# A two-layer graph network on one core: the first layer's own half kept in DRAM and normalised a stage later

## The chip, the cores and the metric

The kernel runs on one core of a Trainium2 chip. The metric is device time in microseconds (us), lower is better. Engines are named as in the profile: PE (matmul) and PEld (its weight loads), DVE (vector), ACT (scalar), POOL (GpSimd) and SP (which only issues DMAs here).

## What is computed

The inputs are x of 12,500 rows by 256, a list of 200,000 edges (src, dst, sorted by dst) with a weight each, and the weights of two layers. Each layer adds its output to x and applies a layer norm. The first layer, cut to what matters here:

```
feat = relu(einsum('nd,ohdk->ohnk', x, W) + b)      # o=0: own half, o=1: neighbour half
att_s = leaky(sum_k feat[0] * a_self)               # 4 heads of 32
att_n = leaky(sum_k feat[1] * a_neigh)
edge_w = (att_s[:, src] + att_n[:, dst]) * weight
agg    = segment_sum(edge_w * feat[1][:, dst], src)
per half and head: (f - mean) * scale * rsqrt(var + 1e-9) + offset
x = layernorm(x + concat(own, agg))
```

The second layer gathers a projected row for each edge, adds the projection of the edge's dst row, applies ReLU, sums by dst, and ends in a matmul, two norms and a residual.

## The kernel before

The edges are cut into tiles of 128, the tiles into 112 groups of 14 (NG = 112, GT = 14). As the edges are sorted by dst, all dst rows of a group lie in one window of 128 rows of x. The nodes are also cut into 98 fixed blocks of 128 rows (NB = 98). Three stages follow each other.

**First stage** (lines 218 to 840). For each group, `sort_tasks` sorts its edges by the block of their src: one-hots of the block of each of the 14 tiles (`widen`, `hot`, `hot_b`, a tile A of 128 x 14 x 99 in bf16), counts per block (`ranks`, 14 matmuls with a column of ones, L600), first rows and places (`begins`, 14 matmuls more, L615; `place_mm`, `place_pick`, L667), and one-hots that permute the edges (`hot_q`, `hot_r`, `goods`, `permute`). The order goes out to DRAM and comes back to all partitions (`rel_out`, `rel_in`, `hot_n`, L725). `message` and `evict` (L734, L741) build a row for each edge from F3, the neighbour half in three bf16 parts, and `scatter` (L747) writes the rows to a log in DRAM, four indirect DMAs a group. The rows lie in a tile m, of which there are three.

For each group, `feat_tasks` makes the features. The neighbour half is needed for the group's window (`xw`), the own half for the block g (`xb`), while there are blocks. So 98 of the 112 steps transpose four squares (L446, L449), copy 512 columns (L455), project both halves from different rows (L467), and then, for the own half, also compute its norm: `offsets` (L460), `square` (L522), `var` (L526), `root` (L529), `rstd` (L532), `norm` (L536), `scale` (L540), `put` (L543). `out_y` stores x + offset + own half in `yd`. The own attention stays in the SBUF tile `atts`.

**The order of the stage is written out by hand.** The table AT gives every task a position; a task of group g stands at 256 g + AT[name]; all tasks are sorted by position and issued in that order. Each engine works through its own instructions in this order, and waits only where data or a buffer is not ready. The `m_` tasks prepare eight groups at a time (their edges' indices and weights).

**Middle stage** (912 to 1116). For each block, its log rows are read in five tiles (`log_load`, `log_hot`, `log_sum`); tile t is summed two steps after its one-hots are made (L958 on DVE, from four `o2` buffers; the multiply L953 on POOL, each fifth tile on DVE; matmuls L966). Log loads are issued nine steps ahead. Blocks are finished in batches of four (the first ones of 1 and 3, the last ones smaller): `load_y` reads the batch's `yd`, `heads_a` to `heads_d` norm the aggregated half (L980 to L1016), then come the layer norm's statistics (L1022), the projection (L1045 to L1059) and the stores. A step is a tile; a batch's tasks stand at steps counted from its first block (b NK, NK = 5) or its end.

**Third stage** (1130 to the end): the second layer, with gathers by POOL (L1286).

Of the kernel before, what the change touches and what calls it, by code (L numbers as in the profile page):

```python
# [11 lines left out]
def _warn_once_fixed(msg, *args, **kwargs):  # L12
# [28 lines left out]
    "widen": -140, "hot": -47, "hot_b": 3, "ranks": 44, "quarter": 71, "rows": 78, "begins": 155,  # L41
    "keep_begins": 189, "keep_v": 180, "shift": 218, "reach": 377, "steps": 314, "steps_keep": 337,
    "steps_low": 358, "target": 474, "index": 554, "place_mm0": 207, "place_mm1": 281, "place_mm2": 370,
    "pick0": 224, "pick1": 255, "pick2": 256, "pick3": 299, "pick4": 305, "pick5": 305, "pick6": 312,
    "pick7": 368, "pick8": 401, "pick9": 408, "pick10": 435, "pick11": 456, "pick12": 457, "pick13": 481,
    "split": 523, "hot_r": 547, "goods": 577, "hot_q": 563, "permute": 636, "rel_keep": 663, "extras": 717,
    "rel_turn": 685, "rel_row": 708, "rel_out": 738, "rel_in": 884, "hot_n": 885, "message0": 965,
    "evict0": 985, "message1": 1004, "evict1": 1046, "message2": 1006, "evict2": 1074, "message3": 1051,
    "evict3": 1132, "message4": 1092, "evict4": 1150, "message5": 1140, "evict5": 1200, "scatter0": 1078,
    "scatter1": 1124, "scatter2": 1163, "scatter3": 1210, "load": -363, "transposes": 234, "keep": 250,  # L50
    "project": 290, "relu": 308, "offsets": 441, "att_mult": 334, "mean_sum": 371, "att_sum": 404,
    "centre": 388, "leaky_n": 494, "part0": 507, "part1": 678, "part2": 741, "part3": 780, "leaky_s": 899,
    "square": 476, "var": 595, "root": 656, "rstd": 792, "norm": 814, "scale": 916, "put": 941, "out_y": 1139,
    "m_load": -1372, "m_cast0": -982, "m_cast1": -1209, "m_col0": -970, "m_keep0": -940, "m_col1": -414,
    "m_keep1": -359, "m_col2": -655, "m_keep2": -607, "m_block": -852, "m_place": -776, "m_high": -348,
    "m_rest": -26, "m_mid": 2, "m_low": 358, "m_win": -179, "m_turn": -654, "m_pairs": -648, "m_mask": -313,
    "m_count": 101,
# [45 lines left out]
def kernel(  # L103
# [45 lines left out]
    yd = dram.tile([ROWS, D], FT, name="yd")  # L149
# [12 lines left out]
    atts = consts.tile([P, NB, H], FT, name="atts")  # L162
# [55 lines left out]
    with ExitStack() as l0:  # L218
# [195 lines left out]
        xb = {}  # L414
        F3 = {}

        def load_group(g):
            if g < NG:
                b = base_reg(g) if g else 0
                xw[g] = xin.tile([P, D], FT, name="xw")  # L420
                nc.sync.dma_start(xw[g], x[bass.ds(b, P), :])
            if g < NB:
                xb[g] = xin.tile([P, D], FT, name="xb")
                n = min(P, N - g * P)
                if n < P:
                    nc.vector.memset(xb[g], 0.0)
                nc.sync.dma_start(xb[g][:n], x[g * P:g * P + n, :])

        def feat_tasks(g):

            ww, bb = g < NG, g < NB
            o0, o1 = (0 if bb else 1), (2 if ww else 1)
            lo, hi = o0 * HD, o1 * HD
            st = {}

            def flat(t):
                return t[:, lo:hi]

            def heads(t):
                return t[:, lo:hi].rearrange("p (a k) -> p a k", k=32)  # L440

            def transposes():
                tp = ps.tile([P, 512], FT, name="tp", bufs=1)
                if ww:
                    for c in range(2):
                        nc.tensor.transpose(tp[:, c * P:(c + 1) * P], xw[g][:, c * P:(c + 1) * P], ident)  # L446
                if bb:
                    for c in range(2):
                        nc.tensor.transpose(tp[:, (2 + c) * P:(3 + c) * P], xb[g][:, c * P:(c + 1) * P], ident)  # L449
                st["tp"] = tp  # L450

            def keep():
                xT = feat.tile([P, 4, P], FT, name="xT")
                a, z = (0 if ww else 2), (4 if bb else 2)
                nc.scalar.copy(xT[:, a:z].rearrange("p c q -> p (c q)"), st["tp"][:, a * P:z * P])  # L455
                st["xT"] = xT

            def offsets():
                st["y"] = feat.tile([P, D], FT, name="y", bufs=3)
                nc.vector.tensor_tensor(st["y"], xb[g], ofb, op=OP.add)  # L460

            def project():
                fp = bank[g][:, 0:D] if ww else ps.tile([P, 512], FT, name="fs")[:, 0:D]
                nc.tensor.matmul(fp[:, lo:hi], ones3, bias3[:, lo:hi], start=True, stop=False)
                for o in range(o0, o1):
                    for c in range(2):
                        nc.tensor.matmul(  # L467
                            fp[:, o * HD:(o + 1) * HD], st["xT"][:, (2 + c) if o == 0 else c, :],
                            w0s[:, c, o * 4:(o + 1) * 4, :].rearrange("p a k -> p (a k)"),
                            start=False, stop=(o == o1 - 1 and c == 1))  # L470
                st["fp"] = fp

            def relu():
                st["R"] = feat.tile([P, D], FT, name="R")
                nc.scalar.activation(flat(st["R"]), st["fp"][:, lo:hi], AF.Relu)

            def att_mult():
                st["tm"] = feat.tile([P, D], FT, name="tm")
                nc.vector.tensor_tensor(flat(st["tm"]), flat(st["R"]),
                                        atb.rearrange("p o h k -> p (o h k)")[:, lo:hi], op=OP.mult)  # L480

            def mean_sum():
                st["m"] = feat.tile([P, 2 * H], FT, name="m")
                nc.vector.tensor_reduce(st["m"][:, o0 * H:o1 * H], heads(st["R"]), AX.X, OP.add)

            def att_sum():
                st["a"] = feat.tile([P, 2 * H], FT, name="a")
                nc.vector.tensor_reduce(st["a"][:, o0 * H:o1 * H], heads(st["tm"]), AX.X, OP.add)

            def centre():  # L490
                st["F"] = feat.tile([P, D + H], FT, name="F", bufs=4)
                m = st["m"][:, o0 * H:o1 * H]
                nc.vector.scalar_tensor_tensor(
                    heads(st["F"]), m[:, :, None].to_broadcast([P, (o1 - o0) * H, 32]), -1.0 / 32, heads(st["R"]),
                    op0=OP.mult, op1=OP.add)

            def leaky_n():
                a = st["a"][:, H:2 * H]
                nc.vector.scalar_tensor_tensor(st["F"][:, D:D + H], a, 0.2, a, op0=OP.mult, op1=OP.max)


            def part(k):
                def f():
                    n = st["F"][:, HD:]
# [11 lines left out]
            def leaky_s():  # L516
                a = st["a"][:, 0:H]
                nc.vector.scalar_tensor_tensor(atts[:, g, :], a, 0.2, a, op0=OP.mult, op1=OP.max)

            def square():  # L520
                st["q"] = feat.tile([P, HD], FT, name="q")
                nc.scalar.activation(st["q"], st["F"][:, 0:HD], AF.Square)  # L522

            def var():
                st["v"] = feat.tile([P, H], FT, name="v")
                nc.vector.tensor_reduce(st["v"], st["q"].rearrange("p (h k) -> p h k", h=H), AX.X, OP.add)  # L526

            def root():
                nc.scalar.activation(st["v"], st["v"], AF.Sqrt, bias=epsh, scale=1.0 / 32)  # L529

            def rstd():
                nc.vector.reciprocal(st["v"], st["v"])  # L532

            def norm():
                c = st["F"][:, 0:HD].rearrange("p (h k) -> p h k", h=H)
                nc.vector.tensor_tensor(c, c, st["v"][:, :, None].to_broadcast([P, H, 32]), op=OP.mult)  # L536

            def scale():
                c = st["F"][:, 0:HD]
                nc.vector.tensor_tensor(c, c, scb[:, 0:HD], op=OP.mult)  # L540

            def put():
                nc.vector.tensor_tensor(st["y"][:, 0:HD], st["y"][:, 0:HD], st["F"][:, 0:HD], op=OP.add)  # L543

            def out_y():
                nc.sync.dma_start(yd[g * P:(g + 1) * P, :], st["y"])

            w = lambda f: f if ww else None
            k = lambda f: f if bb else None
            return dict(transposes=transposes, keep=keep, project=project, relu=relu, offsets=k(offsets),  # L550
# [253 lines left out]
        for g in range(max(NG, NB)):  # L804
            t0 = TG * g
            if g < NG:
                for name, f in sort_tasks(g).items():
                    put_in(t0, name, f)
# [808 lines left out]
```

## Time and profile before

| | |
|---|---|
| Median of 3 runs | 4087.51 us (4082.6 to 4089.36) |
| Profiled execution, its own time | 4089.95 us |
| Its span, first to last instruction | 4088.2 us |
| Mean granted PE clock | 0.989 |
| Busy, share of the span | PE 88%, PEld 74%, DVE 78%, ACT 60%, POOL 62% |
| DMA | 763.85 MB, mean 187 GB/s |

The profile tells for each engine when it was busy, for each group of instructions (line, operation, tile out<-in) the count, the busy time, the mean duration and the idle time just before with what ended it. "L522" is line 522 of the kernel before. A line such as "x98 | 29.9, 306 | 0.0" reads: 98 instructions, 29.9 us busy in all, 306 ns each, no idle time before them.

### The profile page before, as it was taken

The page shows a single profiled execution, that of the slowest core. Times are in us where ns is not written, and L with a number is a line of the kernel's source. Part 1 is how long each engine was busy: PE and PEld are TensorE (multiplying, and loading weights), DVE is VectorE, ACT ScalarE, POOL GpSimd, SP SyncE. Part 2 cuts the span into 40 slices and gives each one's busy share as a digit, 9 for nine tenths or more (in the row PEclk, how much of TensorE's full clock was granted, in tenths as well). Part 3 has the DMA queues.
Part 4 walks back from the last instruction along what each step waited for, and adds up shares of the span by engine and source line. Part 5 has one row for each costly group of instructions (what it writes and reads, how often), then busy time and mean ns, then how long its engine had stood idle before and what let it go on. Part 6 is the DMA issues. An engine that isn't in the chain of part 4 may idle for free.

```text
span 4088.2 us, 86328 instructions
## 1 busy us (share of the span) xinstructions
PE 3580.6 (88%) x26432; PEld 3016.1 (74%) x26432; DVE 3197.3 (78%) x9815; ACT 2465.8 (60%) x8632; POOL 2549.4 (62%) x2461
## 2 busy tenths in 40 slices
PE   7999999999989999999978878787888787787776
PEld 6888888887878888888866666666666666666665
DVE  8999999999878888888856666667666666666666
ACT  7999999999922222222246555555565555555555
POOL 2555555554455555555557777777777777777775
PEclk9999999999999999999999999999999999999999
DMA  5777766665566666666656666666666666666664
GB/s 183 261 259 260 258 221 209 208 209 192 195 204 183 186 185 180 184 186 185 182 148 169 171 171 171 169 171 171 171 170 172 169 173 168 169 173 169 169 171 129
DMA packets 457248, 763.85 MB, mean 187 GB/s; under 512 B 75772, under 2 KB 300574, under 8 KB 456782
## 3 DMA queue, kind: packets, MB, share of 16 engines
q1 hardware_dynamic: 326622, 415.17, 35.7%
q0 software_dynamic: 110848, 327.87, 26.2%
q10 hardware_dynamic: 19312, 15.21, 1.2%
q8 instruction: 216, 3.54, 0.4%
q14 instruction: 250, 2.05, 0.2%
HBM read 553.43 MB, written 204.54 MB: 185 GB/s over the span
## 4 chain that ended last, share of the span: by engine, by line
PE 34%; DMA 24%; DVE 23%; ACT 8%; issue 5%; POOL 4%; DVEq 0%; ACTq 0%; POOLq 0%; SPq 0%
DMA gb<-pd,srcf 21%; PE sum L966 20%; PE agg L1364 6%; DVE gb L1345 4%; POOL gb L1286 4%; ACT gb L1347 3%; DVE mv L685 2%; PE qp L1323 2%; PE qm L1054 2%; ACT junk L667 2%; DVE qh L690 2%; DMA rr<-reld 1%; DVE oT L725 1%; DVE A L592 1%; DMA reld<-rT 1%
## 5 line engine op out<-in xcount | busy, mean ns | idle before, releaser
L1286 POOL DMA_INDIRECT gb<-pd,srcf x1563 | 1510.2, 966 | 511.5 <-issue 266.8
L1364 PE MATMUL agg<-gb,o 128*128 128x256 f32 x3126 | 860.6, 398 | 271.5 <-ACT gb L1347 268.4
L1345 DVE TENSOR_TENSOR gb<-qp,gb 128x512 f32<-128x512 f32 x781 | 538.5, 690 | 653.6 <-DMA gb<-pd,srcf 501.0
L1347 ACT ACTIVATE gb<-gb 128x512 f32<-128x512 f32 x781 | 491.1, 629 | 797.6 <-DVE gb L1345 795.7
L747 POOL DMA_INDIRECT log<-m,ix x448 | 563.6, 1258 | 582.4 <-ACT m L741 386.9
L1364 PEld LDWEIGHTS agg<-gb,o 128*128 128x128 f32 x3126 | 556.0, 191 | 493.2 <-ACT gb L1347 433.3
L966 PE MATMUL sum<-lg,o 128*128 128x256 f32 x3724 | 836.8, 378 | 11.5 <-DVE o L958 11.5
L966 PEld LDWEIGHTS sum<-lg,o 128*128 128x128 f32 x3724 | 696.3, 189 | 109.3 <-POOL lg L953 11.7
L958 DVE TENSOR_SCALAR o<-iotap,lg 128x128 f32<-128x128 f32 x1862 | 627.9, 402 | 123.8 <-PE sum L966 113.8
L953 POOL TENSOR_TENSOR lg<-lg 128x512 f32<-128x512 f32 x392 | 410.3, 1059 | 418.7 <-DMA lg<-log 238.2
L1323 PE MATMUL qp<-qh,oT 128*128 128x256 f32 x1563 | 544.0, 370 | 2.1 <-DVE oT L1310 2.1
L667 ACT ACTIVATE junk<-wp,nbig 128x99 bf16<-128x99 f32 x1568 | 543.5, 352 | 1.9 <-PE wp L640 1.8
L734 PE MATMUL mp<-F,oT 128*128 128x132 bf16 x5376 | 406.4, 221 | 17.5 <-DVE oT L725 13.7
L1323 PE MATMUL qp<-ql,oT 128*128 128x256 f32 x1563 | 406.7, 283 | 0.0
L734 PEld LDWEIGHTS <-oT 128*128 128x128 bf16 x5376 | 349.6, 99 | 47.9 <-DVE oT L725 16.4
L667 ACT ACTIVATION_READ_ACCUMULATOR junk<-wp,nbig 128x1 f32 x1568 | 328.7, 210 | 0.0
L741 ACT COPY m<-mp 128x396 f32<-128x396 f32 (+1 forms) x672 | 313.7, 467 | 14.3 <-PE mp L734 13.9
L1323 PEld LDWEIGHTS qp<-qh,oT 128*128 128x128 f32 x1563 | 299.4, 192 | 20.3 <-DVE oT L1310 2.5
L1323 PEld LDWEIGHTS qp<-ql,oT 128*128 128x128 f32 x1563 | 299.5, 192 | 17.9
L1310 DVE TENSOR_SCALAR oT<-dr,baseP 128x256 fp32r<-128x256 int32 x782 | 288.7, 369 | 10.6 <-DMA dr<-in_dst_dram 10.6
L1331 ACT ACTIVATE o<-iotac,rel 128x128 f32<-128x128 f32 x782 | 266.0, 387 | 1.9 <-issue 1.5
L973 ACT COPY S<-sum 128x256 f32<-128x256 f32 x98 | 36.5, 373 | 337.6 <-PE sum L966 337.6
(253 smaller groups left out, 6429.5 us busy)
## 6 DMA issues: line engine op xcount, KB each, us to landing
lg<-log SPq DMA_DIRECT2D x392, 268.0 KB
dr<-in_dst_dram SPq DMA_DIRECT2D x781, 128.0 KB
rr<-reld SPq DMA_DIRECT2D x112, 512.0 KB
log<-zero SPq DMA_DIRECT2D x101, 268.0 KB
gb<-pd,srcf POOLq DMA_INDIRECT x1563
lg<-log SPq DMA_DIRECT2D x98, 201.0 KB
xw<-in_x_dram SPq DMA_DIRECT2D x112, 128.0 KB
xw<-x1d SPq DMA_DIRECT2D x112, 128.0 KB
```

What stands on the lines that cost most here:

```text
L667: nc.scalar.activation(small("junk", NBX, BF, p=P), st["w", i][:, k * NBE:k * NBE + NBX], AF.Relu, bias=nbig, accum_out=st["sl"][:, t:t + 1])
L734: nc.tensor.matmul(mp[:, r * (HD + H):(r + 1) * (HD + H)], st["oT"][:, r0 + r], F3[g][:, k], start=(k == 0), stop=(k == 2))
L741: nc.scalar.copy(st["m"][:, r0:r0 + n, 0:HD + H], st.pop(("mp", i))[:, :n * (HD + H)].rearrange("p (r w) -> p r w", r=n))
L747: ins = nc.gpsimd.indirect_dma_start(out=log[:, :], out_offset=bass.IndirectOffsetOnAxis(ap=st["ix"][:, k:k + 1], axis=0), in_=st["m"][:, ...
L953: e.tensor_tensor(t[:, 1, :n, 0:HD].rearrange("p r (h k) -> p r h k", h=H), t[:, 0, :n, 0:HD].rearrange("p r (h k) -> p r h k", h=H), t[:, ...
L958: nc.vector.tensor_scalar(o[:, r], iotap, t[:, 0, r, MW - 2:MW - 1], t[:, 0, r, MW - 1:MW], op0=OP.is_equal, op1=OP.mult)
L966: nc.tensor.matmul(sums[b], o[:, r], t[:, :, r, 0:HD], start=(k == 0 and r == 0), stop=(k == NK - 1 and r == n - 1))
L1286: nc.gpsimd.indirect_dma_start(out=gb[s][:r, i], out_offset=None, in_=pd[:, :], in_offset=bass.IndirectOffsetOnAxis(ap=srci[:r, t:t + 1], ...
L1323: nc.tensor.matmul(qp[:r, i], oT[:, i * P:i * P + r], q, start=(k == 0), stop=(k == 1))
L1345: nc.vector.tensor_tensor(z, qp, z, op=OP.add)
L1347: nc.scalar.activation(z, z, AF.Relu)
L1364: nc.tensor.matmul(agg[g], o[:r, i], z[:r, i], start=(j == 0 and i == 0), stop=lastmm)
```

## The change

1. Both halves of the features are made from the group's window alone (`xw`), in each of the 112 groups: two transposes, a copy of 256 columns, one projection to 256 columns. The block rows `xb` are not loaded in this stage.
2. The own half, centred but not normed, and the own attention (4 + 128 columns) are stored to `selfd` in DRAM, at the window's rows (`out_f`). Windows overlap; the rows are the same in both. The norm of the own half leaves the first stage.
3. In the middle stage, `load_y` reads x and `selfd` for the batch, four steps earlier than before and with one y buffer more; `own_s`, `own_b`, `own_r`, `own_c` norm the own half on ACT and DVE; `own_o` and `own_d` add offset and scaled half on POOL. `heads_a` takes the attention from the loaded tile.
4. A new task `pair` adds the one-hots of tiles 0 to 6 to those of tiles 7 to 13; `ranks` and `begins` use the 7 sums in place of the 14 one-hots. (The rank inside such a pair is corrected by the same `twin` count as before.)
5. AT is a new table: all positions are other ones.

```diff
-    "widen": -140, "hot": -47, "hot_b": 3, "ranks": 44, "quarter": 71, "rows": 78, "begins": 155,
...
-    "pick7": 368, "pick8": 401, "pick9": 408, "pick10": 435, "pick11": 456, "pick12": 457, "pick13": 481,
-    "split": 523, "hot_r": 547, "goods": 577, "hot_q": 563, "permute": 636, "rel_keep": 663, "extras": 717,
-    "rel_turn": 685, "rel_row": 708, "rel_out": 738, "rel_in": 884, "hot_n": 885, "message0": 965,
-    "evict0": 985, "message1": 1004, "evict1": 1046, "message2": 1006, "evict2": 1074, "message3": 1051,
-    "evict3": 1132, "message4": 1092, "evict4": 1150, "message5": 1140, "evict5": 1200, "scatter0": 1078,
-    "scatter1": 1124, "scatter2": 1163, "scatter3": 1210, "load": -363, "transposes": 234, "keep": 250,
...
+    "widen": -441, "hot": -264, "hot_b": -242, "pair": -170, "ranks": -117, "quarter": -110, "rows": -57,
...
+    "split": 317, "hot_r": 355, "goods": 410, "hot_q": 351, "permute": 416, "rel_keep": 482, "extras": 488,
+    "rel_turn": 523, "rel_row": 548, "rel_out": 607, "rel_in": 666, "hot_n": 946, "message0": 1022,
+    "evict0": 1062, "message1": 1033, "evict1": 1062, "message2": 1073, "evict2": 1102, "message3": 1078,
+    "evict3": 1112, "message4": 1112, "evict4": 1127, "message5": 1131, "evict5": 1134, "scatter0": 1089,
+    "scatter1": 1117, "scatter2": 1118, "scatter3": 1134, "load": -324, "transposes": 41, "keep": 83,
+    "project": 117, "relu": 146, "att_mult": 220, "mean_sum": 222, "att_sum": 438, "centre": 524,
+    "leaky_n": 659, "part0": 752, "part1": 778, "part2": 848, "part3": 939, "leaky_s": 716, "out_f": 799,
...
             def project():
...
+                fp = st["fp"] = bank[g][:, 0:D]
+                nc.tensor.matmul(fp, ones3, bias3, start=True, stop=False)
+                for c in range(2):
+                    nc.tensor.matmul(fp, st["xT"][:, c, :], w0s[:, c].rearrange("p a k -> p (a k)"),
+                                     start=False, stop=(c == 1))
...
+            def out_f():
+                ins = nc.sync.dma_start(selfd[bass.ds(xreg[g], P), :], st["F"][:, 0:H + HD]).ins
...
-                st["C"] = [st["A"][:, i] for i in range(GT)]
+            def pair():
+                st["B"] = srt.tile([P, h, NBX], BF, name="B")
+                nc.vector.tensor_tensor(st["B"], st["A"][:, :h], st["A"][:, h:], op=OP.add)
+                st["C"] = [st["B"][:, i] for i in range(h)]
...
         def load_y(q):
             b, n = spans[q]
-            ys[q] = bw.tile([P, BB, D], FT, name="y", bufs=3)
-            nc.sync.dma_start(ys[q][:, :n], yd[b * P:(b + n) * P, :].rearrange("(b p) w -> p b w", p=P))
+            y = ys[q] = bw.tile([P, BB, D], FT, name="y", bufs=4)
+            f = fs[q] = bw.tile([P, BB, H + HD], FT, name="fs", bufs=3)
...
+        def own_s(q):
+            b, n = spans[q]
+            own[q] = bw.tile([P, BB, HD], FT, name="oq", bufs=1), bw.tile([P, BB * H], FT, name="ov")
+            nc.scalar.activation(own[q][0][:, :n], fs[q][:, :n, H:], AF.Square)
...
+        def own_b(q):
+            b, n = spans[q]
+            t, v = own[q]
+            nc.vector.tensor_reduce(v[:, :n * H].rearrange("p (b h) -> p b h", h=H),
+                                    t[:, :n].rearrange("p b (h k) -> p b h k", h=H), AX.X, OP.add)
...
+        def own_r(q):
+            b, n = spans[q]
+            v = own[q][1]
+            nc.scalar.activation(v[:, :n * H], v[:, :n * H], AF.Sqrt, bias=epsh, scale=1.0 / 32)
...
+        def own_c(q):
+            b, n = spans[q]
+            v = own.pop(q)[1]
+            F4 = fs[q][:, :n, H:].rearrange("p b (h k) -> p b h k", h=H)
+            nc.vector.reciprocal(v[:, :n * H], v[:, :n * H])
+            nc.vector.tensor_tensor(
+                F4, F4, v[:, :n * H].rearrange("p (b h) -> p b h", h=H)[:, :, :, None].to_broadcast([P, n, H, 32]),
+                op=OP.mult)
...
+        def own_o(q):
+            b, n = spans[q]
+            y = ys[q][:, :n]
+            nc.gpsimd.tensor_tensor(y, y, ofb[:, None, :].to_broadcast([P, n, D]), op=OP.add)
...
+        def own_d(q):
+            b, n = spans[q]
+            F = fs[q][:, :n, H:]
+            nc.gpsimd.tensor_tensor(F, F, scb[:, None, 0:HD].to_broadcast([P, n, HD]), op=OP.mult)
+            y = ys[q][:, :n, 0:HD]
+            nc.gpsimd.tensor_tensor(y, y, F, op=OP.add)
...
-            work[b * NK].append(lambda q=q: load_y(q))
+            t1 = b * NK
+            for d, f in ((-4, load_y), (2, own_s), (3, own_b), (4, own_r), (5, own_c), (1 + n // 2, own_o),
+                         (6 + 2 * (n > 1), own_d)):
+                work[t1 + d].append(lambda q=q, f=f: f(q))
```

## The prediction, made before the changed kernel was run

> **What bounds the kernel now.** I read the table of slices first, then the busy times by stretch, then the groups of each stage by form, the timeline for spacings, and last the waits and the chain. The kernel has three stages one after the other: the first layer's sort and features (0 to about 1143 us), the summing of the log (about 1150 to 2070), and the second layer (to the end). The diff touches the first two. The busy times by stretch (columns: length, then busy us and count for PE, PEld, DVE, ACT, POOL, then clock, DMA share, GB/s):
>
> ```profile
> 100.00:1070.00 970.00, 929.65 (x12097) 804.96 (x12094) 944.55 (x3228) 942.65 (x4639) 499.21 (x390) 0.99 0.68 228
> 1165.00:2060.00 895.00, 895.00 (x4238) 779.34 (x4237) 776.83 (x2303) 192.78 (x449) 463.26 (x430) 1.00 0.63 181
> 2080.00:4088.00 2008.00, 1593.91 (x8256) 1295.15 (x8256) 1317.26 (x3757) 1178.82 (x2846) 1508.90 (x1562) 0.99 0.62 169
> ```
>
> In the first stage three engines are full together: DVE 97.4%, ACT 97.2%, PE 95.8%. A saving on one alone would buy little; the stage shortens by the least of the three. In the middle stage PE is busy without a hole, DVE 87%, ACT 22%, POOL 52%: work put on these three is free as long as PE never waits for it.
>
> Busy is not the sum of durations, because instructions overlap. So I price a DVE or ACT instruction by the distance from its start to the next start, in the timeline:
>
> ```profile
> 708.54 0.28 DVE L540 TENSOR_TENSOR F<-F,scb 128x128 f32<-128x128 f32 x1
> 708.74 0.40 DVE L488 TENSOR_REDUCE a<-tm 128x8 f32<-128x256 f32 x1
> ...
> 709.27 0.28 DVE L543 TENSOR_TENSOR y<-y,F 128x128 f32<-128x128 f32 x1
> 709.47 0.41 DVE L460 TENSOR_TENSOR y<-xb,ofb 128x256 f32<-128x256 f32 x1
> 709.81 0.17 DVE L713 COPY m<-mp 128x16 f32<-128x16 f32 x1
> ```
>
> L540 lasts 0.28 us but holds DVE for 0.20; L460 lasts 0.41 and holds it for 0.34.
>
> **Part 1, what leaves the first stage.** The groups by form (count | busy, mean ns):
>
> ```profile
> L455 ACT COPY xT<-tp 128x512 f32<-128x512 f32 x98 | 56.4, 575 | 0.4 <-PE tp L449 0.4
> L455 ACT COPY xT<-tp 128x256 f32<-128x256 f32 x14 | 5.1, 361 | 0.0
> L529 ACT ACTIVATE v<-v,epsh 128x4 f32<-128x4 f32 x98 | 31.3, 319 | 1.2
> L522 ACT ACTIVATE q<-F 128x128 f32<-128x128 f32 x98 | 29.9, 306 | 0.0
> L588 DVE TENSOR_TENSOR A<-iotab,bx 128x693 bf16<-128x693 bf16 x112 | 57.0, 509 | 0.5 <-ACT bx L584 0.5
> L592 DVE TENSOR_TENSOR A<-iotab,blk 128x693 bf16<-128x693 bf16 x112 | 99.0, 884 | 0.0
> ```
>
> ACT: the copy of the transposes falls to half its width, 98 x (575 - 361) = 21 us. The square (0.21 us to the next start) and the root (0.20) leave: 98 x 0.41 = 40. The table load beside the root (1.3) goes to the middle stage. The last 14 groups now make 256 columns of ReLU instead of 128: 14 x (420 - 319) = 1.4 more. ACT: **-61 us**.
>
> DVE: out go the offsets (0.34), norm, scale and put (0.20 each), the variance sum (0.19) and the reciprocal (0.08): 98 x 1.21 = 119. The last 14 groups widen four operations by 0.13 each and add a leaky of 0.07: +8. The new `pair` adds two bf16 tiles of 128x693. No row shows this sum. Its nearest rows are L588, same shape and type, both inputs plain (0.42 to the next start), and L592, which broadcasts one input (0.80). The sum broadcasts nothing, so I take L588: 112 x 0.42 = 47; the upper end is 90. A gain is excluded: it is an added instruction. DVE: 119 - 8 - 47 = **-64 us**, at worst -21.
>
> PE: 196 transposes leave (37.7 us busy); ranks (L600, 87.8) and begins (L615, 92.5) lose half of their matmuls, 90; the projection's 840 passes of 128 columns (123.7) become 448 of 256 at 0.216 each (the chain has 24 such passes in 5.18 us), 97. PE: **about -155 us**; it drops to some 83% and stops binding.
>
> DVE and ACT fall by nearly the same share, 6%. Over 0 to 1143 us, ACT is busy 1082 and DVE 1086, idle 61 and 57. If the new order leaves as much idle, the stage ends near 1143 - 61 = 1082. The group pitch, (1130.8 - 37.8) / 111 = 9.85 us by the first and last start of L685, becomes about 9.3.
>
> Is the new order as tight? Positions count 256 per group, so one is 36 ns at 9.3 us. I read the two tables against the rows that wait now. `rel_in` to `hot_n` grows from 1 position to 280, and the DVE wait for rr (20 us, 17 times) should go. The pair lies 53 positions (1.9 us) ahead of ranks and takes 0.5. `goods` (1.3 us) is only 6 positions ahead of `permute`, but PE does little between `permute` and the next `message0`, 94 positions on, and now has slack. The ramps: the first group starts 300 positions earlier relative to its scatter, mostly `widen`, hot and pair, which overlap the group before; at the ends a group's own chain (reld out, back, messages, scatters) sets the time, and it is the same. I put 0 to +4 there, take 0.
>
> DMA and queues in this stage: SP issues 98 fewer loads and 14 more stores, the stores 68 KB instead of 128; `out_f` is placed 83 positions behind `leaky_s`, so SP should hardly stop there, and only a load needed 365 positions later stands behind it. `rel_in` now stands 59 positions (2.1 us) behind `rel_out`, so SP will sit for the 2 to 4 us landing that the chain shows for reld; next is a load with the same room. Hidden.
>
> **Part 2, what the middle stage gains.** Per batch of four blocks: ACT a square (0.63) and a root (0.31); DVE a sum (0.68), a reciprocal (0.24) and a multiply (0.69), 1.6 us; POOL the offsets over 128x1024, then a scale and an add over 128x512.
>
> ```profile
> L1014 POOL TENSOR_TENSOR A<-A,scb 128x512 f32<-128x512 f32 x22 | 34.6, 1571 | 0.0
> L1016 POOL TENSOR_TENSOR y<-y,A 128x512 f32<-128x512 f32 x22 | 27.9, 1267 | 1.7
> L958 DVE TENSOR_SCALAR o<-iotap,lg 128x128 f32<-128x128 f32 x1862 | 627.9, 402 | 123.8 <-PE sum L966 113.8 <-DMA lg<-log 8.4
> ```
>
> DVE gets about 40 us in 895, against 118 idle, nearly all of it waiting for PE. POOL gets 1.57 + 1.27 + 2.6 (L1016's slope from 128 to 512 columns, 2.1 ns each, put on L1014) = 5.4 a batch, 133 in all against 432 idle. PE gets nothing. Behind a 2.6 us POOL operation queue the next log multiplies, which PE needs; behind own_b and own_c on DVE, the one-hots. DVE's one-hots run up to four steps ahead (four o2 buffers), each 1.89 us of PE, 7.5 us of lead; the heads, statistics and own work of steps 3 to 11 come to 4.2 + 1.4 us by spacing, while the one-hots of ten steps leave 4.5 free. So PE is not reached: 0. Without that cover it would be 40 us of DVE plus what POOL holds up. The selfd read waits for the last 32 stores, placed 12 us ahead of the scatters that the log waits for anyway. At the start, own_b of the first block stands ahead of tile 4's one-hots, behind six log loads and the new loads on SP; PE then has four tiles, 9.4 us, in hand. I take +1 us, 0 to 3. More bytes: 270 KB a batch, 7 MB, 7 GB/s on 181; hidden.
>
> One row speaks against the change: L1008 over 128x128 lasts 0.29 us at its shortest, but 0.85 when it begins at 1177.08 while POOL's L953 runs from 1176.73 to 1177.78. The Trainium skill (SBUF — State Buffer, Who interferes with whom) states a lock: a DVE instruction with two SBUF inputs and a GpSimd one that reads SBUF exclude each other, and the later one waits to the end. By it, one DVE multiply a batch could stand behind the whole 2.6 us operation, 27 x 2.6 = 70 us more of DVE; with the 40 that reaches its 118 us of idle time. The row alone, 0.56 us each, gives 15.
>
> **The sum.** Made against the profiled execution, 4089.95 us (span 4088.2): 4090 - 61 + 0 + 1 = 4030. The median of the runs is 2.4 below that execution, so I say **4028**.
>
> **Rivals.** (a) The order is looser: ACT needs 9.03 us a group (9.66 busy less 0.63); at 93% busy the pitch is 9.7, the stage gains 16, the time is near 4070. For it: with engines this full, 1% of idle is 11 us, and every position has moved. Against: now PE has room, and today's order holds 97% with none.
>
> (b) The middle stage gives it back: DVE's 40 plus 15 of waits for POOL. If half of it reaches PE, 27 us: 4055; all of it, 4083. Against: 118 idle and the lead.
>
> (c) **Slower**: DVE's `extras` waits for the scatters of three groups before, which still read its buffer (m has three). In the old table `scatter3` lay 275 positions ahead of it, now 122. The evictions are bunched (positions 1062 to 1134, before 985 to 1200), so the scatters follow each other by POOL's own pace: 1.37 us apart at best (563.63, 565.00), up to 2.8. From evict1's end: 0.3 + 3 x 1.37 + 3.3 from issue to landing (1147.35 in the chain; 2.7 to 5.4 elsewhere) = 7.7 us. The table gives 194 positions, 7.0 us, less the copy's 0.4. So it is about 1 us late as placed. DVE can trail ACT by about that once, for all groups, because what PE and ACT take from DVE lies mostly 26 to 90 positions ahead of its use; beyond it, every microsecond comes 112 times. With scatters a further 1 us later: +112 - 61, near 4140. It decides from 0.54 us uncovered a group.
>
> (d) The change doesn't do what it says (the removed work was filler): excluded on ACT and DVE at 97%.
>
> **Chances.** Forecast (4008 to 4046) 0.63; (a) 0.16; (b) 0.08; (c) 0.10; more gain, since PE's slack lifts ACT past 99%, 0.03. Range 4003 to 4072: it takes in the forecast, (a), most of (b) and the pair's upper price where DVE then binds (40 less gained: 4068); (c) and little else is left out. About 0.2%, 8 us, is what the measurement can tell. Faster 0.86 (forecast, more gain, most of a and b), same 0.05, slower 0.09 (c without its mildest part).
>
> **What would show it.** Right: L685's pitch 9.2 to 9.4, ACT and DVE 96% or more in the steady stretch, PE near 84%; `pair` at 0.5 us; PE still without a hole in the middle, POOL near 65%, DVE near 91%. Wrong: DVE waits for "log<-m,ix" before `extras` (c); PE waiting for o or lg in the middle (b); ACT or DVE under 94% (a).

## The result, and the profile after

The changed kernel took **4142.6 us** (median of 4 runs, 4133.08 to 4155.53); beside it the kernel before took 4088.44 us (4082.6 to 4092.74). The ratio is 1.014, interval 1.0123 to 1.0156: slower by 1.4%, where 4028 us was forecast. The profiled execution after took 4133.08 us (span 4131.2), the fastest of its four.

The busy times by stretch of the changed kernel (columns as in the prediction: length, then busy us and count for PE, PEld, DVE, ACT, POOL, then clock, DMA share, GB/s):

```profile
100.00:1070.00 970.00, 856.57 (x9777) 699.75 (x9774) 846.60 (x2656) 861.76 (x4282) 542.83 (x375) 0.96 0.60 204
1200.00:2090.00 890.00, 886.78 (x4183) 770.09 (x4184) 846.58 (x2355) 209.37 (x489) 612.52 (x515) 1.00 0.66 192
2120.00:4131.00 2011.00, 1608.30 (x8271) 1298.37 (x8270) 1320.04 (x3764) 1181.89 (x2860) 1504.71 (x1563) 0.98 0.62 169
```

In the first stage no engine is full any more: DVE fell from 97% to 87%, ACT to 89%, PE to 88%. In the middle stage PE stays full. The loss is in the first stage: the sums of the middle stage (first to last matmul) begin at 1201.0 us, before at 1155.4 (+45.6). They last 910.1 us instead of 907.0 (+3.1), and the rest is 5.6 shorter: together +43.0 (each is rounded), the difference of the spans. The pitch of a group, over groups 10 to 97, is 10.36 us; before it was 9.95.

The waits of the changed kernel between 100 and 1050 us (engine, tile, line, what it waited for: us, times, longest), of which the first was in no such list of the kernel before:

```profile
DVE m L663 <- DMA log<-m,ix: 85.9, 57, 5.6
PEld L684 <- DVE m L664: 71.1, 51, 4.4
PE mp L684 <- DVE m L664: 59.5, 49, 4.2
ACT m L691 <- PE mp L684: 58.6, 51, 4.6
```

L663 and L664 are `extras`, the first writer of a new tile m. DVE stands there until the scatters (log<-m,ix) of three groups before have read the tile. By the profile, PE's message matmuls (L684) then wait for DVE, and ACT's evictions (L691) for PE. The way there is a second buffer: `extras` reads `permute`'s result out of the PSUM tile mp, whose three buffers the message matmuls use too (lines 645 and 681 of the changed kernel), so an `extras` that stands also keeps one of them from PE. This is what the prediction gave as the sign of its case (c).

One such wait, by the timelines of POOL and DVE (start, us, engine, line, operation, the idle time just before):

```profile
557.60 0.96 POOL L697 DMA_INDIRECT log<-m,ix  x1 [1.33 <-ACT v L572]
560.41 1.57 POOL L697 DMA_INDIRECT log<-m,ix  x1 [1.85 <-ACT begun L569]
562.29 1.54 POOL L697 DMA_INDIRECT log<-m,ix  x1 [0.30 <-ACT m L691]
564.13 1.90 POOL L697 DMA_INDIRECT log<-m,ix  x1 [0.30 <-ACT junk L617]
```

```profile
563.68 1.32 DVE L635 TENSOR_TENSOR mv<-rh,em 128x1120 bf16<-128x1120 bf16 x1
564.91 0.29 DVE L488 TENSOR_TENSOR F<-F,F 128x132 bf16<-128x132 f32 x1
565.12 0.75 DVE L675 TENSOR_SCALAR oT<-rr,pcol 128x2048 bf16<-128x2048 bf16 x1
...
566.97 0.41 DVE L455 TENSOR_REDUCE m<-R 128x8 f32<-128x256 f32 x1
568.36 0.19 DVE L663 COPY m<-mp 128x16 f32<-128x16 f32 x1 [0.98 <-DMA log<-m,ix]
```

The last scatter begins 6.5 us after the first, not 4.1 (3 x 1.37) as the prediction had it, and 4.2 us pass from its start to the start of `extras`, not 3.3. DVE has run out of other work at 567.38 and stands for 0.98 us.

### The profile page after: what moved, and what is told of

The parts are those of the page before. It is cut to its first block, busy times and chain, and to the rows that moved or that the text cites. A ratio compares the mean times of both kernels' runs of the same rounds, so it can differ in the third digit from the quotient of the medians.

```text
span 4131.2 us, 81722 instructions
## 1 busy us (share of the span) xinstructions
PE 3552.6 (86%) x24276; PEld 2931.4 (71%) x24276; DVE 3218.8 (78%) x9435; ACT 2436.9 (59%) x8490; POOL 2764.9 (67%) x2542
## 4 chain that ended last, share of the span: by engine, by line
PE 35%; DMA 28%; ACT 13%; DVE 12%; issue 6%; POOL 6%; DVEq 0%; POOLq 0%; ACTq 0%; SPq 0%
DMA gb<-pd,srcf 20%; PE sum L915 19%; DMA log<-m,ix 7%; PE agg L1371 6%; POOL gb L1293 5%; ACT junk L617 4%; DVE gb L1352 3%; ACT gb L1354 3%; PE qp L1330 2%; PE qm L1003 2%; ACT m L691 2%; PE mp L684 1%; DVE qh L640 1%; DVE mv L635 1%; DVE A L538 1%
## 5 line engine op out<-in xcount | busy, mean ns | idle before, releaser
L697 POOL DMA_INDIRECT log<-m,ix x448 | 642.2, 1433 | 549.7 <-ACT v L572 315.3
L915 PE MATMUL sum<-lg,o 128*128 128x256 f32 x3724 | 837.2, 378 | 14.3 <-POOL lg L902 13.2
L907 DVE TENSOR_SCALAR o<-iotap,lg 128x128 f32<-128x128 f32 x1862 | 613.5, 401 | 48.3 <-PE sum L915 37.4
L902 POOL TENSOR_TENSOR lg<-lg 128x512 f32<-128x512 f32 x392 | 435.0, 1123 | 229.4 <-DMA lg<-log 165.8
L684 PE MATMUL mp<-F,oT 128*128 128x132 bf16 x5376 | 410.5, 228 | 70.0 <-DVE m L664 64.5
L684 PEld LDWEIGHTS <-oT 128*128 128x128 bf16 x5376 | 348.8, 101 | 100.1 <-DVE m L664 79.8
L617 ACT ACTIVATION_READ_ACCUMULATOR junk<-wp,nbig 128x1 f32 x1568 | 401.5, 257 | 0.0
L691 ACT COPY m<-mp 128x396 f32<-128x396 f32 (+1 forms) x672 | 302.5, 467 | 71.1 <-PE mp L684 68.5
```

The lines of the kernel that those rows point to most:

```text
L617: nc.scalar.activation(small("junk", NBX, BF, p=P), st["w", i][:, k * NBE:k * NBE + NBX], AF.Relu, bias=nbig, accum_out=st["sl"][:, t:t + 1])
L684: nc.tensor.matmul(mp[:, r * (HD + H):(r + 1) * (HD + H)], st["oT"][:, r0 + r], F3[g][:, k], start=(k == 0), stop=(k == 2))
L691: nc.scalar.copy(st["m"][:, r0:r0 + n, 0:HD + H], st.pop(("mp", i))[:, :n * (HD + H)].rearrange("p (r w) -> p r w", r=n))
L697: ins = nc.gpsimd.indirect_dma_start(out=log[:, :], out_offset=bass.IndirectOffsetOnAxis(ap=st["ix"][:, k:k + 1], axis=0), in_=st["m"][:, ...
L902: e.tensor_tensor(t[:, 1, :n, 0:HD].rearrange("p r (h k) -> p r h k", h=H), t[:, 0, :n, 0:HD].rearrange("p r (h k) -> p r h k", h=H), t[:, ...
L907: nc.vector.tensor_scalar(o[:, r], iotap, t[:, 0, r, MW - 2:MW - 1], t[:, 0, r, MW - 1:MW], op0=OP.is_equal, op1=OP.mult)
```

## The experiments

**T1**: the wait of `extras` for the scatters holds the first stage; without it the changed kernel takes about what was forecast. **T2**, its rival: the time goes to the new order and the new work themselves, and `extras` is only where DVE comes to stand.

Eight of the runs (those said to be at 0.90) were made on two chips that granted PE only some 0.90 of its clock (0.89 to 0.92 over the span), where the kernel before takes 4581 to 4589 us; they are compared with each other and with the kernel before there. The changed kernel itself, with nothing else altered, was not run on them.

**1. A fourth buffer for m, in the changed kernel and in the kernel before.**

```diff
-        msgp = l0.enter_context(tc.tile_pool(name="msgp", bufs=3))
+        msgp = l0.enter_context(tc.tile_pool(name="msgp", bufs=4))
```

> The changed kernel with four buffers of the message tile m in place of three. Theory T1 (rival c of the prediction: extras waits for the scatters of three groups before): the DVE wait for log<-m,ix before extras (103 us, 69 times) falls under 5 us, the PE wait for m behind it (71 us) falls too, the pitch of the groups goes from 10.2 to 9.2-9.5 us, and the time is 4010 to 4050 us. Theory T2 (the new table is loose in other places too, the wait for m only stands where the next wait would stand): the wait moves to another name (index before ranks, place before pick), the pitch stays over 9.8 and the time is 4090 to 4140.

> The kernel before with four buffers of m. T1 and T2 alike: nothing waits for the scatters there, so it is within 0.3% of the kernel before, 4076 to 4100 us. A gain of over 0.5% would say that the buffer helps by itself, and not by what the new table asks of it.

Measured: e1_m4 4030.22 us, ratio to the kernel before 0.9868 (0.9852 to 0.9885); c1_before_m4 4085.62, ratio 1.0005 (0.9995 to 1.0015). `extras` in e1_m4 (durations shortest, median, longest; first and last start; then what its engine stood idle for just before it: us, times):

```profile
L663 DVE COPY m<-mp x112: 166/179/394, 41.3 to 1076.0; 128x16 f32<-128x16 f32 x112
...
  ACT rs L652: 6.3, 16
```

The same two lines of the changed kernel:

```profile
L663 DVE COPY m<-mp x112: 169/186/192, 39.9 to 1177.9; 128x16 f32<-128x16 f32 x112
...
  DMA log<-m,ix: 102.9, 69
```

The wait goes, the last `extras` comes 102 us earlier, the pitch falls to 9.33 us, and the time is 112 us shorter. The kernel before has no use for the buffer. T1 holds; T2, which wanted 4090 to 4140 us, does not.

**2. The new work in the old order**, with three and with four buffers: the old table AT, `pair` at 25, `out_f` at 941.

> The changed kernel with the old table of positions (pair put at 25, out_f at 941), three buffers of m. T1: scatter3 lies 275 positions ahead of extras again, the wait for the scatters is gone, and what was removed shows: 4020 to 4070 us. T2, or a theory T3 (the removed work was not what set the pace): 4080 or more.

> As the run before with four buffers of m. T1: the old table does not ask for the fourth buffer, so the same as with three within 0.3%. If it gains over 0.5%, the scatters are late even with the old table once a group takes less time.

Measured: e2_oldorder 4075.49 us, ratio 0.9977 (0.9967 to 0.9987); e3_oldorder_m4 4070.79, 0.996 (0.9945 to 0.9974). The old order has no wait at `extras` with three buffers, but gains only 9 us, less than T1 expected (4020 to 4070); a fourth buffer changes little, as expected. Its waits between 100 and 1050 us:

```profile
PEld L685 <- DVE oT L676: 53.9, 46, 4.2
DVE oT L676 <- DMA rr<-reld: 51.0, 39, 4.4
PE mp L685 <- DVE oT L676: 46.7, 41, 4.1
```

Here DVE waits for the order's way through DRAM (`rel_in`, one position before `hot_n`), and PE for DVE. With four buffers each, the old table is 41 us slower than the new one (4070.79 and 4030.22). This wait, 53 us in the run with four buffers, is the largest of DVE there; that it makes up the 41 is argued and not shown. The new table is the better one once m has room.

**3. The claim of the buffer moved, with three buffers.** `extras` stays at its position but writes a small tile x2; a new task `extras2`, placed at 1050 (562 positions later), takes m and copies x2 into it.

```diff
+                x2 = st["x2"] = srt.tile([P, NR, 2], FT, name="x2", bufs=4)
+                nc.vector.tensor_copy(x2[:, :, 0], st["go"][:, :, 1])
+                nc.vector.tensor_reduce(x2[:, :, 1], st["go"][:, :, 2:5], AX.X, OP.add)
+            def extras2():
...
-                nc.vector.tensor_copy(m[:, :, MW - 2], st["go"][:, :, 1])
-                nc.vector.tensor_reduce(m[:, :, MW - 1], st["go"][:, :, 2:5], AX.X, OP.add)
+                nc.vector.tensor_copy(m[:, :, MW - 2:], st["x2"])
```

> The changed kernel, new table and three buffers of m as they are; only extras writes its two columns into a small tile of its own, and a new task extras2 at position 1050 copies them into m. So m is taken 562 positions later and the wait for the scatters has room without a further buffer. T1 (extras waits for the scatters, and nothing else of the new table costs): the wait for log<-m,ix is gone, 4025 to 4055 us, at most 20 us over the run with four buffers for the copy (112 small DVE instructions). T2' (the fourth buffer helped for another reason, such as where tiles lie in SBUF): 4100 or more.

> Three buffers of m, taken late (extras by way of a small tile). T1: no wait for log<-m,ix, within 20 us of the run with four buffers. T2': 4100 or more at full clock.

> Three buffers of m, taken late (extras by way of a small tile). At full PE clock, T1: no wait for log<-m,ix, 4025 to 4055 us. T2': 4100 or more. At 0.90 of the clock it was 82 us behind four buffers, without that wait; if that stays at full clock, the small copy or its place costs by itself.

Measured: at full clock (e6_late_m_third) 4033.47 us, ratio 0.9875 (0.9858 to 0.9891); at 0.90 4572.94 (0.9974, 0.9949 to 0.9999) and 4561.8 (0.9967, 0.9949 to 0.9984). At full clock three buffers do as well as four, with one more DVE instruction a group. So neither the number of buffers nor where the tiles lie counts, but that m is claimed before its readers are done. This edit lets go of the PSUM buffer early as well, so what DVE's stand costs by itself, and what the held PSUM buffer adds, is not told apart. At 0.90 the form is worth little, a miss: 4561.8 against 4479.18 for e1_m4_again on the same chip, 83 us where at most 20 were expected. There too `extras` has no wait for the scatters; why the time is lost stays open.

**4. The wait forced on the kernel before**: the same pool with two buffers.

> The kernel before with two buffers of m in place of three: scatter3 then lies 1210 - (717 + 512 - 1210) = only 19 positions ahead of extras two groups on, 0.7 us, and evict5 29. From evict5's end the last scatter needs 0.3 + 1.0 + 2 us to land, so extras is 2 to 3 us late in every group; DVE can trail ACT by about 1 of it. T1: DVE waits for log<-m,ix before extras in most groups, and the time rises by 100 to 250 us. If such a wait is absorbed (T2), under 30 us.

Measured: 4328.15 us, ratio 1.0586 (1.0568 to 1.0604), +243. Its `extras`:

```profile
L713 DVE COPY m<-mp x112: 184/187/192, 46.6 to 1395.0; 128x16 f32<-128x16 f32 x112
...
  DMA log<-m,ix: 221.3, 84
```

The same wait, in a kernel with nothing else changed, gives the same kind of loss: its 221 us of idle time in DVE go with 243 us more, as the 103 in the changed kernel go with 112. (The granted PE clock also fell, from 1.00 to 0.90 between 100 and 1000 us, so a part of the 243 is slower matmuls.)

**5. The end of the chain moved 100 positions earlier**: `leaky_n`, `leaky_s`, `out_f`, `hot_n`, and all of `part`, `message`, `evict` and `scatter`, with three buffers.

> The changed kernel with three buffers of m; only positions are changed: parts, leaky_n, leaky_s, out_f, hot_n, messages, evictions and scatters all stand 100 positions earlier, so that evict1 lies 294 instead of 194 positions ahead of extras. T1: the scatters land in time, the wait is gone and the time falls to 4030 to 4075 us (what the moved tasks now collide with is not planned). If the place of the scatters were not the cause, 4130 or more stays.

Measured, at 0.90: 4770.5 us, ratio 1.0394 (1.0353 to 1.0435). A miss for T1, which wanted a gain; as the changed kernel was not run at 0.90, how much of it the shift costs is not known. `extras` in it:

```profile
L648 DVE COPY m<-mp x112: 184/187/190, 41.8 to 1423.6; 128x16 f32<-128x16 f32 x112
...
  ACT rs L637: 191.5, 81
...
  DMA log<-m,ix: 9.2, 6
```

The wait for the scatters is nearly gone (9 us), but by the profile DVE now stands 191 us at the same place for ACT (rs, the evicted result of `permute`). Moving the chain trades one wait for another; the run says nothing for or against the first wait's price.

**6. Without `pair`, with four buffers**: `ranks` and `begins` use the 14 one-hots again.

```diff
-                st["B"] = srt.tile([P, h, NBX], BF, name="B")
-                nc.vector.tensor_tensor(st["B"], st["A"][:, :h], st["A"][:, h:], op=OP.add)
-                st["C"] = [st["B"][:, i] for i in range(h)]
+                st["C"] = [st["A"][:, i] for i in range(GT)]
```

> The changed kernel with four buffers of m, without pair: ranks and begins use the 14 one-hots again. DVE loses 112 x 0.43 = 48 us, PE gains 14 matmuls a group (about 90 us busy). If DVE and ACT set the pace together and PE has slack, as the prediction has it, the time is the same as with pair within 15 us (ACT still binds at 4020 to 4035). If PE is what the pair relieved, it is 20 to 50 us slower.

> Four buffers of m, no pair. If PE has slack at full clock, within 15 us of the run with four buffers; if the pair relieved PE, 20 to 50 us slower.

> Four buffers of m, no pair. If PE has slack at full clock, within 15 us of 4030; if the pair relieved PE, 20 to 50 us over it. (At 0.90 of the clock it was 101 us over.)

Measured: at full clock (third) **3998.5** us (3994.41 to 4009.97), ratio 0.9795 (0.9776 to 0.9814), the best version there, 32 us below e1_m4, which was not expected. At 0.90 it is the other way round: 4590.49 (1.0007, 0.9989 to 1.0026) and 4580.2 (0.9997, 0.9978 to 1.0017), 101 us above e1_m4_again on the same chip:

> Four buffers of m, once more, as the yardstick for the runs beside it (the last four ran where PE was granted about 0.90 of its clock, and the kernel before took 4589 us there). T1: a ratio to the kernel before of 0.984 to 0.990 if PE has its full clock, 4020 to 4045 us.

Measured: 4479.18 us, ratio 0.9789 (0.9757 to 0.9822). The steady stretch of the first stage, 100 to 1000 us: first e1_m4 at full clock,

```profile
100.00:1000.00 900.00, 856.76 (x10047) 709.12 (x10047) 873.13 (x2733) 870.60 (x4386) 572.48 (x385) 0.97 0.67 225
```

then without `pair` at full clock,

```profile
100.00:1000.00 900.00, 898.89 (x11729) 770.07 (x11729) 859.83 (x2714) 891.01 (x4520) 525.88 (x396) 1.00 0.69 231
```

and without `pair` at 0.90:

```profile
100.00:1000.00 900.00, 823.10 (x9728) 686.40 (x9726) 712.86 (x2238) 762.36 (x3743) 379.70 (x329) 0.93 0.58 196
```

With `pair`, DVE is 97.0% busy and the fullest engine. Without it, DVE has 48 us less to do, ACT reaches 99.0%, and PE, full at 99.9% and at clock 1.00, carries twice the matmuls of `ranks` and `begins`. On the slower PE the same matmuls are dear: ACT falls to 85% and DVE to 79%, and the longest of their waits there are for PE:

```profile
DVE ix L608 <- PE fs L442: 86.9, 41, 2.6
ACT m L689 <- PE fs L442: 60.3, 54, 1.9
```

PE's busy time alone, over groups 10 to 97, is 10.06 us a group there without `pair`, more than the whole pitch of e1_m4_again (9.80). So `pair` trades DVE time for PE time, and on these chips which is wanted went with the clock that was granted.

**7. Without the norm of the own half, with four buffers**: the tasks `own_s` to `own_d` are left out, so the own half is neither normed nor added; its load and the features stay.

> The changed kernel with four buffers of m, the six own tasks of the middle stage left out (the own half is not normed nor added). By the prediction's part 2 they cost 0 to 3 us, so this is within 8 us of the run with four buffers. By rival b (the middle stage gives it back) it is 27 us or more faster.

> Four buffers of m, the six own tasks of the middle stage left out (the own half is not normed nor added). In the last runs the middle stage, from the first to the last matmul of the sums, took 906.7 us without them and 910 to 911 with them, at full clock in that stage. So 3 to 6 us faster than the run with four buffers.

Measured, at 0.90: 4483.46 us (0.9763, 0.9716 to 0.9809) and 4469.67 (0.9765, 0.9707 to 0.9824); beside the second, e1_m4_again took 4479.18. The times overlap (4442 to 4494 against 4475 to 4490), so the stage is read instead: the sums of the middle stage take 907.0 us without this work (906.7 in the first run) and 913.0 with it. Other versions that do this work have 909.5 to 912.5 there, so the moved norm costs some 3 to 6 us where it went.

## Why the prediction was wrong, point by point

**The step that failed** is the 0 that the sum gives the new order, with rival (c) left at 0.10 beside it as "about 1 us late as placed". Its mechanism, its place and its price (near 4140) are what happened; its chance rested on two terms that were too small. "3 x 1.37" for the four scatters took POOL's best spacing, though the same sentence gives up to 2.8: over groups 10 to 94 the median from the first scatter's start to the last one's is 5.69 us, not 4.1. And "3.3 from issue to landing" is 4.19 in the median, from the last scatter's start to `extras`. From the end of `evict1` to `extras` of three groups later it takes 10.36 us in the median, not 7.7; the table leaves 194 positions, 7.0 us at the pitch forecast. That is over 3 us late, not 1. The pitch grows until the loop closes: at 10.36 us the 194 positions are 7.85 us, and DVE trails by the other 2.5. The shorter scatters of before could not be carried over, as the rows before and after show (shortest, median, longest in ns):

```profile
L747 POOL DMA_INDIRECT log<-m,ix x448: 954/1014/3792, 54.7 to 1147.4; - x150
L697 POOL DMA_INDIRECT log<-m,ix x448: 954/1460/3164, 57.1 to 1193.2; - x150
```

The wait does not cause this: in e1_m4, which has no such wait, their median is 1430 ns.

**The conversion was about right.** "Beyond it, every microsecond comes 112 times": DVE stood 103 us for the scatters, 0.92 us a group, and the pitch is 1.02 us longer than in e1_m4 (10.36 against 9.33). That the late chain would come near 4140 us was still luck in part: that price stands for 2 us late with 1 of it covered, and here over 3 us were late and DVE's trailing took up 2.5.

**The work terms of the first stage were about right for ACT and DVE, and wrong for PE.** Three of them, the first two by the groups of the changed kernel, the third of e1_m4 between 100 and 1000 us (count | busy, mean ns | idle before):

```profile
L436 ACT COPY xT<-tp 128x256 f32<-128x256 f32 x112 | 43.3, 387 | 0.0
L542 DVE TENSOR_TENSOR B<-A 128x693 bf16<-128x693 bf16 x112 | 58.0, 518 | 0.1
L442 PE MATMUL fs<-w0s,xT 128*128 128x256 f32 x384 | 108.5, 405 | 0.0
```

`pair` lasts 518 ns and holds DVE for 0.43 us (0.42 taken from L588). Over the stage, taken to end as long before the sums as it did before, e1_m4 has DVE busy 1032 us (1022 by the forecast) and ACT 1017 (1021). PE was forecast to lose 155 us and fall to some 84%. In e1_m4 it is still 95.2% busy: 8.91 us a group where it was 9.57, some 74 us less in all. The 256-column passes, forecast at 0.216 us each, take 0.283 (108.5/384), so the projection saves nothing, where 27 us was forecast; what else is missing stays open.

e1_m4, which has this work and not the wait, took 4030 us, and 4028 was forecast. Its profiled execution, the slowest of its four at 4038.78, shows smaller terms of both signs behind that: its sums begin 54 us earlier than before, not 61, last 5.5 longer, not 1, and the rest is 2.6 shorter, which was not priced.

**Rival (a), a looser order**, did not decide: e1_m4 holds DVE at 97.0% and ACT at 96.7%. It is the old table that is looser for the new work (e3_oldorder_m4, 4071).

**"Now PE has room"** was hardly so (95.2% busy in e1_m4). At full clock DVE is the fullest engine, and leaving out the 48 us that `pair` adds there gained 32, though PE then ran at 99.9%. The prediction had noted that a saving on one of three full engines buys little, and did not ask whether a cost on one that stays full is paid nearly whole.

**The middle stage** was right in outline (PE full, POOL 69% over the stretch, 65% forecast), with DVE at 95%, not 91%. These groups of the middle stage show why (the first one before the change, the others after):

```profile
L1008 DVE TENSOR_TENSOR A<-A,v 128x512 f32<-128x512 f32 x23 | 15.9, 692 | 0.8
L907 DVE TENSOR_SCALAR o<-iotap,lg 128x128 f32<-128x128 f32 x1862 | 613.5, 401 | 48.3 <-PE sum L915 37.4 <-DMA lg<-log 10.3
L902 DVE TENSOR_TENSOR lg<-lg 128x384 f32<-128x384 f32 x98 | 78.4, 800 | 0.0
L957 DVE TENSOR_TENSOR A<-A,v 128x512 f32<-128x512 f32 x23 | 33.7, 1466 | 0.8
L932 DVE TENSOR_TENSOR A<-A,S 128x512 f32<-128x512 f32 x23 | 29.2, 1269 | 0.8
L1063 DVE TENSOR_TENSOR fs<-fs,ov 128x512 f32<-128x512 f32 x23 | 22.6, 983 | 0.8
L929 DVE TENSOR_TENSOR A<-S,fs 128x512 f32<-128x512 f32 x23 | 16.1, 700 | 0.0
```

Several DVE operations with two inputs in SBUF grew: L957 and L932 were 692 ns each before (as L1008 and L983) and L902 637, and the new L1063 was priced at 692, while the one-hots of L907, with one such input, stayed at 401. What decides is whether a POOL operation is running when one begins. Of the 69 instances of L957, L932 and L1063 in 128x512, 54 begin beside one and last up to 1.66 us; their ends lie 0.55 us after the end of that operation or of the POOL operation next to it. The other 15 begin beside none and last 0.69, as did all 46 of L1008 and L983 before. L929, with two inputs as well, begins beside none in 22 of 23 cases and keeps its 0.68. The sum of the growth is 23 x (774 + 577 + 291) + 98 x 163 ns = 54 us. The row priced this at 15, for one multiply a batch, where three operations and L902 grew; the lock that the Trainium skill states (SBUF — State Buffer, Who interferes with whom) was worked out to 70 as an estimate, and the run is nearer to that and shows the lock itself. DVE's idle time took most of it: the middle stage grew by 3 to 5.5 us, still more than the 1 forecast. PE's one long wait there (13.2 us at the start, for POOL's first multiplies) stands beside one of 11.5 before, which is 1.7 of the changed kernel's 3.1 us; where the rest comes from stays open.

## What to carry to other kernels

When an order is moved, go through the buffers as well as the engines: for each, count the positions from its last reader to its next writer, turn them into time at the new pitch, and set against that the last reader's chain with durations as they are in that crowded place, not at their best. A late claim of 1 us on an engine that is full is paid in every iteration, and one buffer more is the whole cure (4143 to 4030 us here); a claim put later in the order did as well at full clock (4033), but not at 0.90. Where several engines are full together, work taken from one and put on another is priced by the fuller one, and at the clock that the chip grants.

## What the runs showed of the hardware that was not expected

**The scatters stretch beside some DVE work.** In the kernel before, 85 scatters begin while DVE runs the products mv (L685 there); the 68 of them that meet no wide one-hot oT last 0.96 us in the median, and the 17 that do last 2.4 us and end while it runs. After the change 99 begin beside mv (L635), and the wide one-hot oT (L675, a tensor_scalar in bf16) follows mv closely while every one of them still runs: 1.9 us in the median, as in the last one shown above, and all end 0.12 to 0.18 us after oT. The Trainium skill (SBUF — State Buffer, Who interferes with whom) says that DMA whose descriptors GpSimd makes can be held up by DVE in a two-port mode, which tensor_scalar can enter and tensor_tensor cannot. These rows agree, but no run here took oT away, so the cause is argued and not shown. Nor can it be the whole: 174 scatters of the changed kernel have no tensor_scalar, copy or cast beside them and still last 1.53 us in the median, against 0.99 for the 197 such ones before. What stretches those stays open.

**The granted PE clock differed between the versions in the first stage, mostly with PE's busy time.** Before the change it was 1.00 between 100 and 1000 us with PE busy 96%; e1_m4, 95% busy, has 0.97, the changed kernel 0.96 at 88%, the kernel before with two buffers 0.90 at 86%, and without `pair`, 99.9% busy, 1.00. It is not strict: the old order with the new work has 0.98 at 91%. On one of the two other chips e1_m4 had 0.95 and the version without `pair` 0.93 in the same stretch, and 0.86 and 0.87 in the third stage, and there the order of the two versions turned round. But the middle stage, where PE is busy without a hole, ran at 1.00 there as well (e1_m4_again, 1300 to 2000 us): what is called 0.90 here is a mean over stages.
